# A Perceiver layer on one core: the order and the queues of the first loads

## Chip, core and metric

The kernel runs on one core of a Trainium2 chip. The metric is the device time of one execution in microseconds, as a median of several runs. A profile of one execution comes with it; its span is counted from the first to the last instruction.

## What is computed

Four batches of 256 tokens of width 256 pass through one layer with three parts, all in fp32:

```python
# x: (4, 256, 256), ctx: (4, 4096, 256)
q = layernorm(x) @ Wq1                       # 8 heads of 64
k = concat(layernorm(x) @ Wk1, ctx @ Wk2)    # 256 + 4096 keys
v = concat(layernorm(x) @ Wv1, ctx @ Wv2)
x = x + softmax(q k^T / 8) v @ Wo + bo       # cross attention
x = x + routed(layernorm(x))                 # top quarter of the tokens: attention; the others: a state space model
x = x + experts(layernorm(x))                # mixture of 8 experts, 2 per token
```

The constants spoken of below (`ln_w`, `r_w1`, `conv_w`, `A_log` and so on) belong to the routed part. The cross attention needs of the constants only its own weights and `bo`.

## The kernel before

**Cross attention in passes.** A group G is one batch and one pair of heads: 16 groups, four for each batch. For a group, the keys are made from eight chunks of ctx with 512 tokens each (`k_chunk`, L872): a load of 512 KB into one of four `ctx` buffers (L801), matmuls with `wk2` (L879) into one of three PSUM banks with tag "m", and a copy to `kt` on ScalarE (`keys_out`, L867). `k_self` (L885) adds the keys of x itself and the queries (L892, weights `wself`, held in one buffer). `v_chunk` (L902) makes the values from the same chunks of ctx, loaded a second time (L916). The norm of a batch (`norm`, L834) is done on VectorE and ScalarE, with `bo` added to `x_sb` by POOL (L842); `turn_x` (L845) transposes it on TensorE (L850) and copies it on ScalarE (L854).

**The first group.** The keys of group 0 come ahead of the loop: chunk 0, the norm of batch 0, chunks 1 to 7 with `turn_x` after chunk 4, then `k_self` (L1059 to L1066). Under `manual_schedule` each engine executes its instructions in the order in which the program writes them.

**The loop.** L1069 runs over n, 8 steps for each group: scores of step n (L932, L940), exponentials of step n - 1 on ScalarE (L980), maxima on VectorE (L952), transposes on VectorE (L989), values times weights on TensorE (L998). Between them lie pieces that make the next data: steps 2 to 4 of a group make its values (nine chunks), steps 6, 7 and 0 the keys of the next group. Loads of ctx are written at the place where the chunk is made, and SyncE's queue runs ahead of the other engines until no buffer is free. In step 0 of a group, `wk` and `wself` for the next group are loaded ahead of the first ctx chunk.

**The planner.** Work other than that is written as generators. `start(g)` puts one on a list; `slot(budget)` (L738), called three or four times in each step, lets each generator on the list go one step if the planner's clock `now[0]` has come to its due time and its cost fits in the budget. A generator yields the time to its next step and that step's cost. The clock is advanced by estimates (2.1 for the scores, 1.75 or 1.95 for a piece), not by measured times. `finish_batch` and, after it, `routed` start on this list when the fourth group of a batch has been through the loop, for batch 0 at about n = 34.

**The loads at the start.** `load_qk(0)` and `load_self(0)` go on SyncE's queue. On ScalarE's queue go x of all four batches (L809), `xbo` (L71), `xwo` (L815), and in `load_consts` (L88) 16 loads: `abo`, `r_w1`, `r_w2`, nine columns (L77), `r_b2`, `conv_w`, `xproj_w` and `A_log`. `load_consts` also computes with them (`bqs`, the exponential of `A_log`, `w2b`) and makes masks and indices on POOL. These two parts are written ahead of the `manual_schedule` block.

Of the kernel before, what the change touches and what calls it, by code (L numbers as in the profile page):

```python
# [8 lines left out]
F32 = mybir.dt.float32  # L9
# [5 lines left out]
P = 128  # L15
B, T, D = 4, 256, 256
# [27 lines left out]
def perceiver_layer(ctx: ExitStack, tc: tile.TileContext, a: dict, out: bass.AP):  # L44
# [23 lines left out]
    def row_bc(name):  # L68

        t = const.tile([P, D], F32, name=f"{name}_bc")  # L70
        nc.scalar.dma_start(out=t, in_=a[name].partition_broadcast(P))  # L71
        return t

    def col(name, n):

        t = const.tile([P, n], F32, name=f"{name}_col")
        nc.scalar.dma_start(out=t, in_=a[name].rearrange("(c p) -> p c", p=P))  # L77
        return t

    def rows(name, n, m):  # L80

        t = const.tile([P, n, m], F32, name=f"{name}_sb")
        nc.scalar.dma_start(out=t, in_=a[name].rearrange("(c p) m -> p c m", p=P))
        return t

    cs = {}

    def load_consts():  # L88

        cs["abo"] = row_bc("abo")  # L90
        cs["r_w1"] = rows("r_w1", KD, P)
        cs["r_w2"] = rows("r_w2", 1, 1)
        for name, n in (
            ("ln_w", KD), ("ln_b", KD), ("r_b1", 1), ("bq", KD), ("bk", KD), ("bv", KD),
            ("conv_b", NDT), ("dt_b", NDT), ("Dp", NDT),
        ):
            cs[name] = col(name, n)
        t = cs["r_b2"] = const.tile([P, 1], F32, name="r_b2_bc")
        nc.scalar.dma_start(out=t, in_=a["r_b2"].partition_broadcast(P))
        bqs = cs["bqs"] = const.tile([P, KD], F32, name="bqs")  # L100
        nc.vector.tensor_scalar_mul(bqs, cs["bq"], AHD ** -0.5)
        cs["conv_w"] = rows("conv_w", NDT, DC)
        cs["xproj"] = rows("xproj_w", NDT, DTR + 2 * DS)

        amat = cs["amat"] = rows("A_log", NDT, DS)
        nc.scalar.activation(amat, amat, AF.Exp)
        nc.vector.tensor_scalar_mul(amat, amat, -1.0)
        w2b = cs["w2b"] = const.tile([P, P], F32, name="w2b")
        nc.vector.tensor_copy(w2b, cs["r_w2"][:, 0, :].to_broadcast([P, P]))

        tri = cs["tri"] = const.tile([P, P], F32, name="tri")
        nc.gpsimd.affine_select(
            out=tri, in_=ones, compare_op=ALU.is_gt, fill=0.0, base=0,
            pattern=[[1, P]], channel_multiplier=-1,
        )
        tokid = cs["tokid"] = const.tile([P, 2], F32, name="tokid")
        nc.gpsimd.iota(
            tokid, pattern=[[P, 2]], base=0, channel_multiplier=1,
            allow_small_or_imprecise_dtypes=True,
        )  # L120
        posid = cs["posid"] = const.tile([P, T], F32, name="posid")
        nc.gpsimd.iota(
            posid, pattern=[[1, T]], base=0, channel_multiplier=0,
            allow_small_or_imprecise_dtypes=True,
        )

        hm1 = const.tile([P, 8], F32, name="hm1")
        hmask = cs["hmask"] = const.tile([P, 8], F32, name="hmask")
        nc.gpsimd.affine_select(
            out=hm1, in_=ones[:, :8], compare_op=ALU.is_ge, fill=0.0, base=0,  # L130
            pattern=[[-AHD, 8]], channel_multiplier=1,
        )
        nc.gpsimd.affine_select(
            out=hmask, in_=hm1, compare_op=ALU.is_gt, fill=0.0, base=AHD,
            pattern=[[AHD, 8]], channel_multiplier=-1,
        )

        vbd = cs["vbd"] = const.tile([P, AH // 2, 2, AHD], F32, name="vbd")
        nc.gpsimd.memset(vbd, 0.0)

    def moments(src):
        n = src.shape[1]
# [631 lines left out]
    with ExitStack() as s1:  # L774
# [14 lines left out]
        def load_qk(G):  # L789
            return load_weights(G, ("wk2",), "wk2", 2)  # L790

        def load_self(G):
            return load_weights(G, ("wk1", "wq1"), "wself", 1)
# [10 lines left out]
            )  # L804
            return t

        wqk, wself, wv = {0: load_qk(0)}, {0: load_self(0)}, {}
        for b in range(B):
            nc.scalar.dma_start(  # L809
                out=x_sb[:, 2 * b : 2 * b + 2, :],  # L810
                in_=a["x"][b].rearrange("(h p) d -> p h d", p=P),
            )
        bo_bc = row_bc("xbo")
        wo = fin.tile([P, NHC, D], F32, name="xwo_sb")
        nc.scalar.dma_start(out=wo, in_=a["xwo"].rearrange("(c p) m -> p c m", p=P))  # L815
        load_consts()

        same = fin.tile([P, 4, 32], F32, name="same")
        dm = same[:, 0, :]
# [52 lines left out]
        def k_chunk(G, g):  # L872
            b = G // NHP
            if G not in kts:
                kts[G] = wk.tile([P, 4, QK], F32, tag="kt", name="kt")
            ct = load_ctx(b, g)
            ps = ps_m.tile([P, 512], F32, tag="m", name="psk")
            for c in range(KD):
                nc.tensor.matmul(  # L879
                    ps, wqk[G][:, 0, c, :], ct[:, c, :],  # L880
                    start=(c == 0), stop=(c == KD - 1),
                )
            keys_out(G, g * (CK // 4), ps)
# [173 lines left out]
        with tc.manual_schedule():  # L1057
            norms = {}
            k_chunk(0, 0)  # L1059
            for _ in norm(0):  # L1060
                pass
            for g in range(1, NCH):
                k_chunk(0, g)
                if g == 4:
                    turn_x(0)
            k_self(0)  # L1066
            wv[0] = load_v(0)
            N = 8 * NG
            for n in range(N + 2):  # L1069
                G, s = divmod(n, 8)  # L1070
                new, old = n < N, 1 <= n <= N


                pieces, took = [], 1.75
                if s == 5 and G + 1 < NG:
                    wv[G + 1] = load_v(G + 1)
                if s % 4 == 1:
                    m, took = n // 4 - 1, 1.95
                    if m >= 0:
                        pieces = [  # L1080
                            lambda i=i: values(m, i, min(i + 9, NJ)) for i in range(0, NJ, 9)
                        ]
                elif 2 <= s <= 4 and G < NG:
                    pieces = [
                        lambda g=g: v_chunk(G, g) for g in range(3 * s - 6, 3 * s - 3)
                    ]
                elif G + 1 < NG:
                    if s == 0:
                        wqk[G + 1] = load_qk(G + 1)
                        wself[G + 1] = load_self(G + 1)  # L1090
                    pieces = {
                        0: [lambda g=g: k_chunk(G + 1, g) for g in range(3)],
                        6: [lambda g=g: k_chunk(G + 1, g) for g in range(3, 6)],
                        7: [lambda: k_self(G + 1)]
                        + [lambda g=g: k_chunk(G + 1, g) for g in range(6, 8)],
                    }[s]

                def piece(i):
                    if i < len(pieces):
                        pieces[i]()  # L1100
                        now[0] += took

                if new:
                    scores(n)
                    now[0] += 2.1
                if old:
                    exps(n - 1)
                if new:
                    copy_max(n)
                piece(0)  # L1110
                if s % 4 != 1:
                    slot(0.5)
                    piece(1)
                    if old:
                        turn(n - 1, 0)
                    if new:
                        stat(n)
                        now[0] += 0.3
                    if old:
                        turn(n - 1, 1)  # L1120
                    slot(0.5)
                    piece(2)
                    slot(2.9)
                else:
                    slot(1.5)
                    piece(1)
                    if new:
                        stat(n)
                        now[0] += 0.3
                    slot(2.8)  # L1130
                    piece(2)
                    slot(1.5)
                    piece(3)
                    if old:
                        turn(n - 1, 0)
                        turn(n - 1, 1)
                b = n // 32 + 1
                if b < B:
                    if n % 32 == 20:
                        norms[b] = norm(b)  # L1140
                    if n % 32 in (20, 22):
                        next(norms[b])
                    if n % 32 == 29:
                        turn_x(b)
# [443 lines left out]
```

## Time and profile before

| | us |
|---|---|
| median of 3 runs (1651.16 to 1979.53) | 1652.6 |
| profiled execution | 1654.12 |
| its span | 1652.4 |
| TensorE matmul busy | 1502.1 (91%) |
| VectorE busy | 1027.0 (62%) |
| ScalarE busy | 757.6 (46%) |
| POOL busy | 454.3 (27%) |
| mean DMA traffic | 135 GB/s |
| end of the last matmul of the first `k_self` | 42.05 |

In the profile PE is TensorE's matmul, PEld its weight load, DVE VectorE, ACT ScalarE, POOL GpSimd, SP SyncE; ACTq and SPq are the instruction queues of ScalarE and SyncE where they issue loads. L with a number is a line of the kernel. `out<-in` names the written and the read tile, `xN` counts instructions. A line of waits reads: who waited, for whom, us in total, how many times, longest. A line of the chain of waits gives start, length and what the time was spent on.

### The profile page before, as it was taken

The page shows a single profiled execution, that of the slowest core. Times are in us where ns is not written, and L with a number is a line of the kernel's source. Part 1 is how long each engine was busy: PE and PEld are TensorE (multiplying, and loading weights), DVE is VectorE, ACT ScalarE, POOL GpSimd, SP SyncE. Part 2 cuts the span into 40 slices and gives each one's busy share as a digit, 9 for nine tenths or more (in the row PEclk, how much of TensorE's full clock was granted, in tenths as well). Part 3 has the DMA queues.
Part 4 walks back from the last instruction along what each step waited for, and adds up shares of the span by engine and source line. Part 5 has one row for each costly group of instructions (what it writes and reads, how often), then busy time and mean ns, then how long its engine had stood idle before and what let it go on. Part 6 is the DMA issues. An engine that isn't in the chain of part 4 may idle for free.

```text
span 1652.4 us, 37317 instructions
## 1 busy us (share of the span) xinstructions
PE 1502.1 (91%) x15724; PEld 1079.1 (65%) x15724; DVE 1027.0 (62%) x1721; ACT 757.6 (46%) x1481; POOL 454.3 (27%) x591
## 2 busy tenths in 40 slices
PE   5899999999999999999999999999876697766799
PEld 2557667576857667686757576756654586666587
DVE  0556666567469996655899866469894313444353
ACT  2444454446566663646675445566542133222211
POOL 1000000000427871040678400427573161000110
PEclk8999999999999999999999999999987697787799
DMA  5453443443444542523454443344401364542361
GB/s 172 147 170 110 151 144 106 155 146 102 137 149 145 162 156 85 180 94 117 152 177 146 125 135 103 132 152 139 122 15 58 134 227 163 185 146 90 105 226 45
DMA packets 157687, 223.41 MB, mean 135 GB/s; under 512 B 14896, under 2 KB 76080, under 8 KB 157520
## 3 DMA queue, kind: packets, MB, share of 16 engines
q1 hardware_dynamic: 142928, 208.15, 39.0%
q10 hardware_dynamic: 13104, 8.81, 1.9%
q0 software_dynamic: 1488, 4.07, 0.8%
q8 instruction: 124, 2.03, 0.5%
q14 instruction: 43, 0.35, 0.1%
HBM read 216.56 MB, written 4.42 MB: 134 GB/s over the span
## 4 chain that ended last, share of the span: by engine, by line
PE 79%; DVE 12%; DMA 3%; issue 2%; ACT 2%; POOL 1%; SPq 1%; ACTq 0%; DVEq 0%; POOLq 0%
PE psv L916 15%; PE po L998 14%; PE su L932 13%; PE psk L879 11%; PE su L940 2%; DVE sp L952 2%; PE yps L665 2%; DMA ctx<-in_ctxT 2%; PE p1b L1403 2%; DVE db L582 2%; PE pdb L1417 2%; PE pg L1510 2%; PE pu L1510 2%; PE pde L1522 2%; DVE pt L989 2%
## 5 line engine op out<-in xcount | busy, mean ns | idle before, releaser
L952 DVE TENSOR_SCALAR_CACHE_REDUCE sp<-su 128x1088 f32<-128x1088 f32 x256 | 318.7, 1281 | 170.3 <-PE su L940 170.1
L989 DVE STREAM_TRANSPOSE pt<-sp 128x1088 f32<-128x1088 f32 x256 | 327.9, 1295 | 81.6 <-PE po L998 81.3
L980 ACT ACTIVATE sp<-sp,nb 128x1088 f32<-128x1088 f32 x256 | 305.2, 1195 | 3.8 <-DVE nb L969 3.6
L879 PE MATMUL psk<-ctx,wk 128*128 128x512 f32 x512 | 249.6, 621 | 23.2 <-ACT kt L867 9.3
L998 PE MATMUL po<-pt,v 128*64 128x128 f32 x4352 | 261.0, 278 | 3.6 <-DVE pt L989 3.5
L932 PE MATMUL su<-kt,qz 64*32 64x512 f32 x4096 | 255.1, 606 | 2.8 <-DVE nb L969 2.0
L916 PE MATMUL psv<-wv,ctx 128*128 128x128 f32 x2048 | 251.2, 279 | 0.0
L998 PEld LDWEIGHTS po<-pt,v 128*64 128x64 f32 x4352 | 242.6, 139 | 9.4 <-issue 4.7
L916 PEld LDWEIGHTS psv<-wv,ctx 128*128 128x128 f32 x2048 | 236.1, 192 | 7.8 <-issue 3.2
L879 PEld LDWEIGHTS psk<-ctx,wk 128*128 128x128 f32 x512 | 92.1, 194 | 110.8 <-issue 80.5
L920 ACT COPY v<-psv 128x512 f32<-128x512 f32 x144 | 80.3, 560 | 162.3 <-PE psv L916 161.9
L932 PEld LDWEIGHTS su<-kt,qz 64*32 64x32 f32 x4096 | 63.1, 107 | 121.5 <-issue 88.8
L589 POOL TENSOR_TENSOR db<-db,cb 128x384 f32<-128x384 f32 x96 | 106.9, 1114 | 115.5 <-DVE db L582 88.4
L582 DVE TENSOR_TENSOR_SCAN db<-da,db 128x192 f32<-128x192 f32 x192 | 136.3, 769 | 0.0
L591 POOL TENSOR_TENSOR y<-y,db 128x192 f32<-128x192 f32 x192 | 122.1, 636 | 15.1
L867 ACT COPY kt<-psk 128x512 f32<-128x512 f32 x128 | 73.8, 583 | 110.8 <-PE psk L879 110.5
L572 ACT ACTIVATE da<-delta,A_log_sb 128x192 f32<-128x192 f32 x192 | 75.9, 447 | 97.5 <-DVE db L582 95.7
L460 POOL TENSOR_SCALAR xc<-xi,conv_w_sb,conv_b_col 128x192 f32<-128x192 f32 x16 | 8.0, 497 | 390.6 <-ACT xi L492 214.1
L940 PEld LDWEIGHTS su<-kt,qz 128*32 128x32 f32 x2048 | 34.7, 110 | 109.7 <-issue 109.7
L577 POOL TENSOR_TENSOR db<-bb,xc 128x384 f32<-128x384 f32 x96 | 96.4, 1028 | 0.2
L1251 DVE SCALAR_TENSOR_TENSOR sg<-sg,p0b 128x512 f32<-128x512 f32 x19 | 13.1, 687 | 124.5 <-ACT sg L1250 124.5
L665 PE MATMUL yps<-db,ident 128*128 128x192 f32 x128 | 38.2, 466 | 49.9 <-DVE db L663 49.9
(274 smaller groups left out, 1686.3 us busy)
## 6 DMA issues: line engine op xcount, KB each, us to landing
ctx<-in_ctxT SPq DMA_DIRECT2D x256, 512.0 KB, 4.6
gateT<-in_gateT SPq DMA_DIRECT2D x27, 512.0 KB, 3.9
upT<-in_upT SPq DMA_DIRECT2D x27, 512.0 KB, 8.1
downT<-in_downT SPq DMA_DIRECT2D x27, 512.0 KB, 5.7
bb<-bcd SPq DMA_DIRECT2D x24, 192.0 KB, 4.9
cb<-bcd SPq DMA_DIRECT2D x24, 192.0 KB, 5.2
wv<-in_wv SPq DMA_DIRECT2D x32, 128.0 KB, 2.3
in_w<-in_in_w SPq DMA_DIRECT2D x24, 128.0 KB, 3.3
```

The lines of the kernel that those rows point to most:

```text
L577: nc.gpsimd.tensor_tensor(db, bbs[k], bc(xc[:, m, :], 1, SG), ALU.mult)
L582: nc.vector.tensor_tensor_scan(out=db[:, s, :], data0=da[:, s, :], data1=db[:, s, :], initial=0.0, op0=ALU.mult, op1=ALU.add,)
L589: nc.gpsimd.tensor_tensor(db, db, cbs[k], ALU.mult)
L591: nc.gpsimd.tensor_tensor(y[:, m, :], y[:, m, :], db[:, s, :], ALU.add)
L879: nc.tensor.matmul(ps, wqk[G][:, 0, c, :], ct[:, c, :], start=(c == 0), stop=(c == KD - 1),)
L916: nc.tensor.matmul(ps[:, i * P : (i + 1) * P], lhsT, wv[G][:, w, c, :], start=(c == 0), stop=(c == KD - 1),)
L920: nc.scalar.copy(v.rearrange("p k d -> p (k d)"), ps[:, : n * P])
L932: nc.tensor.matmul(su[q * 32 : (q + 1) * 32, SC[j] + lo : SC[j] + lo + 512], qT[r, j, s * 32 : (s + 1) * 32], kt[r, q, lo : lo + 512], sta ...
L952: nc.vector.tensor_scalar(out=sps[n][j], in0=su[:, SU[j] : SU[j] + QK], scalar1=1.0, scalar2=None, op0=ALU.mult, op1=ALU.max, accum_out=nm ...
L980: nc.scalar.activation(sps[n][j], sps[n][j], AF.Exp, bias=nbs[n][:, j : j + 1], accum_out=lss[b][:, hp, s, j : j + 1],)
L989: nc.vector.transpose(pts[m, j][:, i, :], sps[n][j])
L998: nc.tensor.matmul(pos[m][j * HD : (j + 1) * HD, :], vts[m // 2, k // 4][:, k % 4, j * HD : (j + 1) * HD], pts[m, j][:, :, kk * 32 : (kk + ...
```

## The change

Ahead of the first matmul only these loads are issued: `wk2` of the first pair of heads (SyncE's queue), x of batch 0 (ScalarE's queue) and ctx. `wself` follows the first ctx chunk on SyncE's queue, and `xbo` follows the first key copy on ScalarE's. x of batches 1 to 3, `xwo` and the 16 constants become a generator `load_later`, which is started on the planner's list ahead of the loop. Each of its steps issues one load on SyncE's queue, and a last step, 8 units of the planner's clock after the last load, does the arithmetic on the constants. What POOL makes is put in `make_consts`, called where `load_consts` was.

```diff
     def row_bc(name):
...
-        nc.scalar.dma_start(out=t, in_=a[name].partition_broadcast(P))
+        nc.sync.dma_start(out=t, in_=a[name].partition_broadcast(P))
...
     def col(name, n):
...
-        nc.scalar.dma_start(out=t, in_=a[name].rearrange("(c p) -> p c", p=P))
+        nc.sync.dma_start(out=t, in_=a[name].rearrange("(c p) -> p c", p=P))
...
     def rows(name, n, m):
...
-        nc.scalar.dma_start(out=t, in_=a[name].rearrange("(c p) m -> p c m", p=P))
+        nc.sync.dma_start(out=t, in_=a[name].rearrange("(c p) m -> p c m", p=P))
...
+    def make_consts():
...
     def load_consts():
 
-        cs["abo"] = row_bc("abo")
         cs["r_w1"] = rows("r_w1", KD, P)
+        yield 1.0, 0
         cs["r_w2"] = rows("r_w2", 1, 1)
+        yield 1.0, 0
         for name, n in (
             ("ln_w", KD), ("ln_b", KD), ("r_b1", 1), ("bq", KD), ("bk", KD), ("bv", KD),
             ("conv_b", NDT), ("dt_b", NDT), ("Dp", NDT),
         ):
             cs[name] = col(name, n)
+            yield 1.0, 0
         t = cs["r_b2"] = const.tile([P, 1], F32, name="r_b2_bc")
-        nc.scalar.dma_start(out=t, in_=a["r_b2"].partition_broadcast(P))
+        nc.sync.dma_start(out=t, in_=a["r_b2"].partition_broadcast(P))
+        yield 1.0, 0
+        cs["conv_w"] = rows("conv_w", NDT, DC)
+        yield 1.0, 0
+        cs["xproj"] = rows("xproj_w", NDT, DTR + 2 * DS)
+        yield 1.0, 0
+        amat = cs["amat"] = rows("A_log", NDT, DS)
+        yield 1.0, 0
+        cs["abo"] = row_bc("abo")
+        yield 8.0, 0.5
         bqs = cs["bqs"] = const.tile([P, KD], F32, name="bqs")
         nc.vector.tensor_scalar_mul(bqs, cs["bq"], AHD ** -0.5)
-        cs["conv_w"] = rows("conv_w", NDT, DC)
-        cs["xproj"] = rows("xproj_w", NDT, DTR + 2 * DS)
-
-        amat = cs["amat"] = rows("A_log", NDT, DS)
+
         nc.scalar.activation(amat, amat, AF.Exp)
         nc.vector.tensor_scalar_mul(amat, amat, -1.0)
         w2b = cs["w2b"] = const.tile([P, P], F32, name="w2b")
         nc.vector.tensor_copy(w2b, cs["r_w2"][:, 0, :].to_broadcast([P, P]))
...
-        wqk, wself, wv = {0: load_qk(0)}, {0: load_self(0)}, {}
-        for b in range(B):
-            nc.scalar.dma_start(
+        wqk, wself, wv = {0: load_qk(0)}, {}, {}
+
+        def load_x(b):
+            (nc.sync if b else nc.scalar).dma_start(
                 out=x_sb[:, 2 * b : 2 * b + 2, :],
                 in_=a["x"][b].rearrange("(h p) d -> p h d", p=P),
             )
-        bo_bc = row_bc("xbo")
+
+        load_x(0)
+        make_consts()
+        bo_bc = const.tile([P, D], F32, name="xbo_bc")
         wo = fin.tile([P, NHC, D], F32, name="xwo_sb")
-        nc.scalar.dma_start(out=wo, in_=a["xwo"].rearrange("(c p) m -> p c m", p=P))
-        load_consts()
+
+        def load_later():
+
+            for b in range(1, B):
+                load_x(b)
+                yield 2.0, 0
+            nc.sync.dma_start(out=wo, in_=a["xwo"].rearrange("(c p) m -> p c m", p=P))
+            yield 2.0, 0
+            yield from load_consts()
...
             k_chunk(0, 0)
+            wself[0] = load_self(0)
+            nc.scalar.dma_start(out=bo_bc, in_=a["xbo"].partition_broadcast(P))
             for _ in norm(0):
                 pass
...
             k_self(0)
+            start(load_later())
             wv[0] = load_v(0)
```

More of the change, by code (lines that the diff above doesn't have):

```diff
@@ L82, in rows @@
         t = const.tile([P, n, m], F32, name=f"{name}_sb")
-        nc.scalar.dma_start(out=t, in_=a[name].rearrange("(c p) m -> p c m", p=P))
+        nc.sync.dma_start(out=t, in_=a[name].rearrange("(c p) m -> p c m", p=P))
         return t
     cs = {}
-    def load_consts():
-        cs["abo"] = row_bc("abo")
[L91 to L98, printed above, removed]
-        nc.scalar.dma_start(out=t, in_=a["r_b2"].partition_broadcast(P))
-        bqs = cs["bqs"] = const.tile([P, KD], F32, name="bqs")
-        nc.vector.tensor_scalar_mul(bqs, cs["bq"], AHD ** -0.5)
-        cs["conv_w"] = rows("conv_w", NDT, DC)
-        cs["xproj"] = rows("xproj_w", NDT, DTR + 2 * DS)
-        amat = cs["amat"] = rows("A_log", NDT, DS)
[L106 to L109, printed above, removed]
+    def make_consts():
         tri = cs["tri"] = const.tile([P, P], F32, name="tri")
@@ L139, in load_consts @@
         nc.gpsimd.memset(vbd, 0.0)
+    def load_consts():
+        cs["r_w1"] = rows("r_w1", KD, P)
+        yield 1.0, 0
+        cs["r_w2"] = rows("r_w2", 1, 1)
+        yield 1.0, 0
+        for name, n in (
+            ("ln_w", KD), ("ln_b", KD), ("r_b1", 1), ("bq", KD), ("bk", KD), ("bv", KD),
+            ("conv_b", NDT), ("dt_b", NDT), ("Dp", NDT),
+        ):
+            cs[name] = col(name, n)
+            yield 1.0, 0
+        t = cs["r_b2"] = const.tile([P, 1], F32, name="r_b2_bc")
+        nc.sync.dma_start(out=t, in_=a["r_b2"].partition_broadcast(P))
[8 more added lines that the diff above has]
+        yield 8.0, 0.5
+        bqs = cs["bqs"] = const.tile([P, KD], F32, name="bqs")
+        nc.vector.tensor_scalar_mul(bqs, cs["bq"], AHD ** -0.5)
+        nc.scalar.activation(amat, amat, AF.Exp)
+        nc.vector.tensor_scalar_mul(amat, amat, -1.0)
+        w2b = cs["w2b"] = const.tile([P, P], F32, name="w2b")
+        nc.vector.tensor_copy(w2b, cs["r_w2"][:, 0, :].to_broadcast([P, P]))
     def moments(src):
```

## The prediction

> **What bounds the kernel now.** I read the page's first part, then the busy times by stretch, then the chain of waits of the first 60 us, then the timelines of the two queues that issue loads. The busy times by stretch:
>
> ```profile
> core 0: us, PE busy (x) PEld busy (x) DVE busy (x) ACT busy (x) POOL busy (x), PEclk, DMA share, GB/s
> 0.00:60.00 60.00, 36.09 (x180) 14.91 (x188) 10.24 (x29) 17.43 (x29) 4.30 (x18) 0.88 0.60 184
> 60.00:360.00 300.00, 299.20 (x3708) 204.76 (x3700) 188.38 (x297) 139.51 (x246) 2.40 (x4) 1.00 0.41 131
> ```
>
> TensorE is the bound from 60 us on (299.2 of 300 us busy). Only the first 60 us have holes, 24 us of them. The chain of waits shows what fills them:
>
> ```profile
> 4.61 8.35 DMA ctx<-in_ctxT
> ...
> 17.44 4.07 DMA ctx<-in_ctxT
> 21.51 0.02 issue
> 21.53 0.37 ACTq L83
> 21.91 0.04 issue
> 21.95 4.62 DMA A_log_sb<-in_A_log
> ...
> 40.31 1.74 PE psks L892 x8
> ```
>
> The columns are start and length in us. The first keys end at 42.05 us, and before that the chain runs over the list of constants on ScalarE's queue. That list must be issued before ScalarE can do its first copy out of PSUM, as its timeline shows:
>
> ```profile
> 8.89 1.25 ACTq L83 DMA_DIRECT2D r_w_sb<-in_r_w  x2
> ...
> 21.95 1.71 ACTq L83 DMA_DIRECT2D A_log_sb<-in_A_log  x1
> 23.68 1.28 ACT L867 ACT_TABLE_LOAD   x1 [23.68 <-DMA Dp_col<-in_Dp]
> 24.98 0.59 ACT L867 COPY kt<-psk 128x512 f32<-128x512 f32 x1
> ```
>
> The first chunk's matmuls ended at 12.76 us; their copy starts at 24.98 us. Three banks of PSUM are full by 17.44 us, and TensorE stands still from there to 25.62 us. SyncE's queue is held too; its waits up to 130 us include these:
>
> ```profile
> SPq L801 <- DMA r_w_sb<-in_r_w: 9.8, 1, 9.8
> SPq L801 <- DMA dt_b_col<-in_dt_b: 4.0, 1, 4.0
> SPq L801 <- DMA x_sb<-in_x: 3.7, 3, 1.8
> ```
>
> The issue of a ctx chunk waited for loads of the other queue to land.
>
> [...] a matmul L879 takes 0.94 us at first (4 in 3.75) and 0.44 later (12 in 5.32), the weight loads fall from 0.33 to 0.19 us after 14.02 us, and after the hole it is slow again (4 in 3.78 at 25.62 and at 30.56). [...] the trace has both queues sharing 345 to 381 GB/s between 4.5 and 8 us. [...]
>
> **The change part by part.**
>
> *Fewer bytes ahead of the first matmul.* Now it starts at 9.01 us, by when x of four batches (1024 KB), three weights (384 KB), ctx chunk 0 (512 KB) and most of a row constant (128 KB) have moved. After, it needs wk (128 KB), x of one batch (256 KB, sharing the engines) and chunk 0 (512 KB): 0.92 MB. The bandwidth in slices of 0.75 us from 1.5 us on is 28, 145, 309, 367, 360 GB/s, which sum to 0.91 MB at 5.25 us. About 0.3 us lies between the last bytes and the matmul (2.05 MB are reached near 8.7 us, the matmul starts at 9.01). Start 5.6 us: 3.4 us gained.
>
> *From the first matmul to the end of the first own keys (L892).* Now 42.05 - 9.01 = 33.0 us. After, ScalarE has one load (xbo, 0.35 us) behind the first copy. TensorE has 32 matmuls L879, four transposes and the L892 group. Of the first 12 matmuls about six were slow (3.75 + 4.43 us against 12 x 0.443 = 5.3 leaves 2.9 us excess, 0.5 each). So 6 x 0.94 + 26 x 0.443 + 0.82 + 1.74 = 19.7 us with no hole. Is it fed? ScalarE: copy 0 at 9.4 to 10.0, xbo to 10.4, square-root table 11.7, root 12.0, VectorE 0.4, two scalings 1.1 to 13.5, copy 1 to 14.1, copy 2 to 14.7. Chunk 3 needs copy 0, chunk 4 (due at 15.7) copy 1, the transposes (17.5) copy 2 and the scaled x: all in time, by 1.6 us or more. ctx: chunks 1 to 3 follow wself at about 350 GB/s, landing near 7.7, 9.6 and 11 us against 9.4, 12.1 and 13.9; chunks 4 to 7 wait for their buffer and land about 3.9 us after chunks 0 to 3 end, 13.3 at the earliest against 15.7. End: 5.6 + 19.7 = 25.3 us; 13.3 us gained here. Taken together 16.7 us.
>
> *x of batches 1 to 3 and wo on SyncE's queue.* The planner's steps put x1 and x2 between the three ctx loads of step n = 0, x3 in n = 1, wo in n = 2. Now TensorE waits at 45.1 to 46.97 us for the first of those chunks, which is late because wself, in one buffer, can only be reloaded after L892. That wait stays. Each 256 KB is 0.7 us at 370 GB/s; chunk two then lands near 48.9 us in the old time against 48.8 due, chunk three near 51.1 against 50.9: a cost of 0.3 us (0 to 1.5). x3 and wo (another 2.1 us) fall into the stretch to 62 us where SyncE has run ahead to full buffers: nothing.
>
> *Sixteen small loads, between steps n = 2 and 7.* They have 0.35 to 1.71 us of issue each or for a pair, 9.0 us in all by ScalarE's timeline, on a queue that spends 53 us of 60 to 130 us waiting:
>
> ```profile
> SPq L801 <- PE psv L916: 16.5, 3, 11.1
> SPq L801 <- PE psk L879: 13.5, 4, 8.5
> SPq L783 <- PE psv L916: 10.5, 1, 10.5
> ```
>
> These waits are for TensorE to free a buffer; they are the cover. What is behind a small load is the next ctx load: it is issued about 8.1 us ahead of its use (buffer of value chunk 0 free at 64.0, chunk 4 due at 72.1) and takes 5.6 us to land, so 2.5 us are spare. One small load's issue (0.5 us) and bytes fit. I take zero, bounds 0 and 3 us; uncovered, the 9.0 us would count in full.
>
> *The closing step* (exponential 0.26 us on ScalarE, three VectorE operations of 0.6 us together) moves to n = 8, where VectorE and ScalarE are under two thirds busy: zero, at most 0.6 us. The POOL constants move earlier on an engine that nobody waits for: zero. The planner's clock counts no time for the loads, and the list is used up before the router starts near n = 35: the later order stays.
>
> *Sum.* -3.4 - 13.3 + 0.3 = -16.4 us. The span goes from 1652.4 to 1636.0 us; the profiled run (1654.1 us) would give 1637.7. The median shown is 1652.6, 1.5 below that run, so the prediction is 1636.2 us, 1.0% faster.
>
> **The rivals.**
> 1. *A new hole in the first pass.* If the table load ahead of copy 0 only starts once chunk 0 is ready (1.3 us), the norm's ScalarE work delays copies 1 and 2 to 15.4 and 16.0 us, near their due times; a ctx chunk late by 2 us on top lets the clock fall back, and eight matmuls cost 0.5 us more each. Together 1.3 + 2 + 8 x 0.5 = 7.3 us of the gain go: 1643.5 us. For it: a short hole at 29.4 kept the clock low until 34 us. Against it: the margins above.
> 2. *SyncE's queue becomes the bound in n = 3 to 7.* If two small loads had to land (2.8 us each, as bv_col took) before the next ctx load proceeds, that load would come 5.6 + 5.6 - 8.1 = 3.1 us late; about 11 ctx loads have such neighbours, 34 us in all, and the time would be 1670 us, slower than before. It decides from a lateness of 1.5 us a chunk. For it: the 9.8 and 4.0 us waits shown. Against it: nine small loads were issued at 15.5 to 19.2 us, 0.4 to 0.5 us apart, without waiting for each other to land.
> 3. *A little more.* [...] 1 us is saved; if the hole at 54.9 to 57.7 us no longer drops it (32 matmuls L932 took 3.19 us after it, 1.88 later), another 1.3: 1634 us. Most of this is in the likeliest case's range.
>
> **How the numbers follow.** The likeliest case has 0.70 and a range of 1631 to 1641 us ([...] the x loads 1.2, spread between runs 1.5 to 3). Rival 1 has 0.15, rival 2 has 0.06, rival 3 0.06, and 0.03 is for a change in the later stages that no view shows. The range from 1628 to 1648 takes in rivals 1 and 3. Two per cent, about what a measurement can tell from no change, is 33 us. All but parts of rival 2 and of the rest lie within: faster 0.03, same 0.93, slower 0.04.
>
> **What would show it right or wrong.** Right: first matmul near 5.6 us, copy 0 near 9.4, no hole over 1 us among L879, L892 ending near 25 us, the hole before n = 1 as before, TensorE over 99% busy from 45 us on. Wrong: matmuls L879 at 0.94 us beyond the first eight; TensorE waiting for ctx with SyncE's queue held by a constant; TensorE busy below 98% between 45 and 120 us.

## The result, and the profile after

| | before | after | difference | predicted |
|---|---|---|---|---|
| median, us | 1651.2 | 1637.3 | -13.9 | -16.4 |
| ratio (95% interval) | | 0.9916 (0.9896 to 0.9936) | | 0.990 |
| first matmul of the keys, us from the start | 9.01 | 5.75 | -3.3 | -3.4 |
| end of the first own keys | 42.05 | 24.67 | -17.4 | -16.7 |
| start of the first value matmul | 62.0 | 45.8 | -16.2 | -16.4 |
| span of the profiled execution | 1652.4 | 1633.2 | -19.2 | -16.4 |

The median of before has one more run in it than the one shown with the prediction. The slow run of 1979.5 us is left out of it here, and out of the ratio. The new time lies in the predicted range (1631 to 1641 us). The change is small, 0.84%, but the interval keeps it clear of no change: it goes from 11 to 17 us.

The chain of waits of the kernel after, over the same stretch (start, length, what):

```profile
1.31 4.30 DMA ctx<-in_ctxT
5.61 0.14 issue
5.75 3.56 PE psk L902 x4
...
22.93 1.74 PE psks L915 x8
...
26.64 5.75 DMA ctx<-in_ctxT
32.39 0.14 issue
32.52 1.95 PE psk L902 x4
...
45.89 4.08 PE psv L939 x32
```

No ScalarE list stands in it any more. The one thing that is longer than before lies behind the own keys: the chain is in ctx loads until 32.39 us. The second ctx load of step n = 0 now stands behind an x load and takes 5.75 us to land, and TensorE waits for it a second time (1.1 us). ScalarE's timeline shows what the copies were freed of:

```profile
1.34 1.28 ACT L890 ACT_TABLE_LOAD   x1 [1.34 <-PEq L1602]
...
9.33 0.59 ACT L890 COPY kt<-psk 128x512 f32<-128x512 f32 x1 [6.71 <-PE psk L902]
9.34 0.39 ACTq L1084 DMA_DIRECT2D xbo_bc<-in_xbo  x1
9.94 1.28 ACT L168 ACT_TABLE_LOAD   x1
```

The first copy follows its matmuls at once (24.98 us before). The first table load runs while ScalarE has nothing else to do, so the dependence on chunk 0 that the first rival feared is not there. In the steps where the constants are issued, SyncE's queue waits for TensorE, as it did before; its longest waits up to 130 us:

```profile
SPq L812 <- PE psv L939: 34.3, 6, 14.0
SPq L812 <- PE psk L902: 19.1, 10, 4.0
```

**Why 16.2, 19.2 and 13.9 us are one gain.** At the copy of the first finished values (L1009 before, L1032 after) the gain is 16.0 us; at the tenth such copy it is 15.9 us (409.20 and 393.29). Then it grows in jumps, in steps where the two kernels have the same work, to 17.4 at the eighteenth and 18.9 at the nineteenth. Busy times in the stretch of the last of these jumps, first before, then after (the third number from the end is the granted clock of TensorE as the profile gives it, 1.00 for full speed):

```profile
717.00:766.00 49.00, 48.20 (x570) 39.18 (x576) 23.91 (x37) 27.20 (x57) 20.32 (x33) 0.97 0.34 115
```
```profile
700.00:747.00 47.00, 46.20 (x568) 37.63 (x560) 23.60 (x37) 26.86 (x57) 20.32 (x33) 1.00 0.36 120
```

TensorE idles for 0.8 us in both, and the clock was 0.97 against 1.00. By estimate, three per cent of 48 us is about 1.5 us, the whole jump. I take the jumps to belong to these two executions, though this clock is shown for the last one alone: the other executions of the changed kernel have spans of 1635.6 to 1637.0 us, two to four above the profiled one. What the traces show of the change is the 16 us of the start; the medians show 13.9, with an uncertainty of about 3.

### The profile page after: what moved, and what is told of

Its sections match the earlier page's. It is cut to its first block, busy times and chain, and to the rows that moved or that the text cites. A ratio compares the mean times of both kernels' runs of the same rounds, so it can differ in the third digit from the quotient of the medians.

```text
span 1633.2 us, 37319 instructions
## 1 busy us (share of the span) xinstructions
PE 1494.2 (91%) x15724; PEld 1075.6 (66%) x15724; DVE 1026.8 (63%) x1721; ACT 757.5 (46%) x1481; POOL 454.0 (28%) x591
## 4 chain that ended last, share of the span: by engine, by line
PE 79%; DVE 11%; DMA 4%; issue 2%; ACT 1%; POOL 1%; SPq 1%; ACTq 0%; POOLq 0%; DVEq 0%
PE psv L939 15%; PE po L1021 14%; PE su L955 13%; PE psk L902 11%; PE su L963 3%; DVE sp L975 2%; DMA ctx<-in_ctxT 2%; PE yps L676 2%; PE p1b L1429 2%; DVE db L593 2%; PE pdb L1443 2%; PE pg L1536 2%; PE pu L1536 2%; PE pde L1548 2%; DVE pt L1012 2%
## 5 line engine op out<-in xcount | busy, mean ns | idle before, releaser
L902 PE MATMUL psk<-ctx,wk 128*128 128x512 f32 x512 | 244.9, 611 | 12.5 <-DMA ctx<-in_ctxT 11.1
```

What stands on the lines that cost most here:

```text
L902: nc.tensor.matmul(ps, wqk[G][:, 0, c, :], ct[:, c, :], start=(c == 0), stop=(c == KD - 1),)
```

## The experiments

Two places are followed in each trace: the first matmul of the keys, and the start of the first value matmul, which is free of what happens in the remaining 1590 us. Each is one execution. Ratios are to runs of the kernel before that were made beside the experiment, each with its interval.

| run | first matmul | first value matmul | median, us | ratio |
|---|---|---|---|---|
| before | 9.01 | 62.0 | 1651.2 | 1 |
| after | 5.75 | 45.8 | 1637.3 | 0.9916 (0.9896 to 0.9936) |
| e1_defer_x | 6.31 | 47.5 | 1637.9 | 0.9907 (0.9891 to 0.9924) |
| e2_wself_step1 | 6.17 | 42.2 | 1629.2 | 0.9858 (0.9842 to 0.9874) |
| e3_burst | 6.43 | 54.3 | 1644.0 | 0.9945 (0.9929 to 0.9962) |
| e4_scalar_steps | 5.87 | 46.3 | 1638.5 | 0.9928 (0.9904 to 0.9952) |
| e5_x_all_first | 6.44 | 46.0 | 1638.1 | 0.9930 (0.9904 to 0.9957) |
| e6_list_after_keys | 8.86 | 63.1 | 1653.4 | 1.0006 (0.9996 to 1.0017) |
| e7_both | 5.32 | 42.3 | 1629.4 | 0.9863 (0.9846 to 0.9880) |
| e8_wself_first | 7.31 | 48.6 | 1638.9 | 0.9910 (0.9892 to 0.9927) |
| e9_wself_x_first | 9.53 | 52.2 | 1641.4 | 0.9925 (0.9909 to 0.9942) |
| e10_before_wself_step1 | 9.29 | 58.3 | 1645.1 | 0.9955 (0.9938 to 0.9972) |

### Is it enough to move the list? (e6)

```diff
-        load_consts()
...
             k_self(0)
+            load_consts()
```

> Edit of the kernel before: only the list of 16 constants (loads and arithmetic, on ScalarE's queue, in one go) is moved from the start to behind the first own keys. My theory: the list on ScalarE's queue held the first key copies, so the keys now end near 28.5 us instead of 42.1 (first matmul still near 9 us), but ScalarE then issues 9 to 17 us before it can copy the keys of the next group, so a part comes back as a hole in steps n = 0 and 1: first value matmul at 56 to 62 us, time 1646 to 1651 us. Rival, that the bytes of the start and not ScalarE's list are what counted: the keys end at 40 us or later.

The keys end at 28.0 us, so the list did hold the first copies: moving it alone takes 14 us off them. But the time is that of before. ScalarE's timeline in this run:

```profile
28.06 0.40 ACTq L71 DMA_DIRECT2D abo_bc<-in_abo  x1
...
42.25 1.28 ACT L106 ACT_TABLE_LOAD   x1 [13.15 <-DMA Dp_col<-in_Dp]
46.71 0.26 ACT L106 ACTIVATE A_log_sb<-A_log_sb 128x64 f32<-128x64 f32 x1 [3.18 <-DMA A_log_sb<-in_A_log]
46.99 1.07 ACT L865 COPY kt<-psk 128x512 f32<-128x512 f32 x2
```

Here the list with its arithmetic lasts from 28.06 to 46.97 us, 19 us, and the next copy of keys waits behind it. I had expected some of the gain to remain; all of it went. From the end of the own keys to the first value matmul it is 35.1 us against 20.0 before: 15 us are lost where 14 were gained. In one piece the list costs about as much behind the own keys as ahead of them; what makes the change pay is that it is cut up.

### One load in each step, or all at once? (e3)

```diff
-            start(load_later())
+            rest = load_later()
+            for due, cost in rest:
+                if cost:
+                    break
+            active.append([rest, 60.0, 0.5])
```

> Edit: all 20 late loads are issued in one go on SyncE's queue after the first own keys, ahead of step n = 0, instead of one in each planner step; the closing arithmetic stays near step n = 8. My theory: SyncE's queue stands idle from 16 to 24.7 us, waiting to reload wself, and the burst (about 11 us of issue) falls mostly into this gap. ctx of step 0 is then issued near 27.5 us instead of 25.6, but without x between its chunks: L939 at 46.5 us (45.8 before), the first 32 us of steps no slower, time 1638 us. Rival, that spreading the loads is what makes the change free: every load in the burst delays ctx, L939 at 54 us or later, time 1645 us or more.

I had expected 46.5 us at the value matmuls and 1638 us; it is 54.3 and 1644.0, as the rival had it. SyncE's timeline in this run:

```profile
18.30 1.80 SPq L83 DMA_DIRECT2D r_w_sb<-in_r_w  x2
...
23.68 0.37 SPq L77 DMA_DIRECT2D bk_col<-in_bk  x1
25.12 0.37 SPq L77 DMA_DIRECT2D bv_col<-in_bv  x1
...
29.27 0.50 SPq L71 DMA_DIRECT2D abo_bc<-in_abo  x1
...
32.34 11.37 SPq L812 DMA_DIRECT2D ctx<-in_ctxT  x6
```

The 20 loads last from 16.3 to 29.8 us, 13.5 us where I had counted 11, because some of them wait for earlier loads to land (from 24.05 to 25.12 us for wo). ctx of step 0 is issued at 32.34 us instead of 25.62, 6.7 us late. TensorE stands still for 9.0 us, the granted clock is 0.50 from 32 to 37.4 us and 0.62 from 37.5 to 43, and the value matmuls start 8.4 us late. So spreading matters on SyncE's queue too: these 8 us are what the planner's steps hide.

### Does it matter which queue has the constants? (e4)

```diff
-        nc.sync.dma_start(out=t, ...)      # row_bc, col, rows, r_b2
+        nc.scalar.dma_start(out=t, ...)
```

> Edit: the 16 constants are issued in the same planner steps but on ScalarE's queue instead of SyncE's (x of batches 1 to 3 and wo stay on SyncE's). My theory: their place, not their queue, gives the gain; ScalarE spends the 9 us of issue in its idle time in steps n = 2 to 7. Start of the first value matmul 45.8 us and end of the first group's values as in the changed kernel within 0.5 us, time 1637 us. Rival, that the constants on SyncE's queue cost ctx loads some time in steps n = 2 to 7: 1 to 3 us faster. Rival, that the queue is what matters: some 8 us slower.

The value matmuls start 0.5 us later, the first values are finished at 77.62 us (77.48 after), and the intervals of the two ratios overlap for the most part. Cut into steps, the constants can be on either queue. The second half of the change's description, that SyncE issues them, is not where the gain is.

### Which bytes held the first matmul? (e5, e8, e9)

e5 loads x of all batches ahead of the first matmul again, on ScalarE's queue; e8 puts wself ahead of ctx again, on SyncE's; e9 does both.

```diff
-        load_x(0)
+        for b in range(B):                 # e5, e9: on ScalarE's queue
+            load_x(b)
...
-        wqk, wself, wv = {0: load_qk(0)}, {}, {}
+        wqk, wself, wv = {0: load_qk(0)}, {0: load_self(0)}, {}    # e8, e9
```

> Edit: x of all four batches is loaded ahead of the first matmul on ScalarE's queue, as in the kernel before; everything else as changed. My theory: 768 KB more ahead of ctx chunk 0 at 350 GB/s is 2.2 us: first matmul at 8.0 us instead of 5.75, end of the first own keys at 26.9 instead of 24.7 us, and step n = 0 gets 1.1 us back since no x lies between its ctx loads: L939 at 46.9 us, time 1638 us. Rival: x on the other queue doesn't delay ctx on SyncE's, and the first matmul starts at 5.8 us.

> Edit: the changed kernel with wself of group 0 back ahead of ctx chunk 0 on SyncE's queue, as in the kernel before. Five runs with the same start as the changed kernel had their first matmul at 5.75 to 6.43 us (mean 6.1), and x of all batches on ScalarE's queue ahead of it (e5) only moved it to 6.44. My new theory: what held the first matmul before was not x on the other queue but the two weights ahead in the same queue, whose issue is 1.0 us and whose 256 KB come first: first matmul at 7.6 us, end of the first own keys about 1.5 us later than 24.7. Rival: the order on SyncE's queue doesn't count either, first matmul at 6.1 us, and what held it is xbo and wo or all of them together.

> Edit: e8 and e5 together: wself ahead of ctx chunk 0 on SyncE's queue, x of all batches on ScalarE's. Theory that wself alone counts: first matmul at 7.6 us as in e8. Rival, that the bytes of x count once the ctx load is issued late, so that both queues' bytes go ahead of it: 8.5 to 9.0 us as in the kernel before. Time in both cases 1637 to 1641 us, since ctx chunks and banks have more slack then.

Five runs with the start of the changed kernel (after, e1 to e4) begin at 5.75 to 6.43 us, mean 6.1. 768 KB of x more move this to 6.44 only, hardly outside that spread, and not to 8.0: my reason for the first term fails. wself ahead makes 7.31 us, close to the 7.6 expected. With both it is 9.53 us, 3.4 us late, more than 0.3 and 1.2 together. That is as late as with the whole start of the kernel before (8.86 to 9.29 us in before, e6 and e10), though xbo and wo come late in e9: they are not needed for it. The ctx load in e8 and e9, issued at the same moment:

```profile
2.33 4.85 DMA ctx<-in_ctxT
```
```profile
2.33 7.06 DMA ctx<-in_ctxT
```

Issued at 1.31 us, ctx lands after 5.0 us even with x of four batches on the other queue (e5). Issued at 2.33 us, when ScalarE's queue is at the last of those four x loads (they are issued from 0.81 to 2.88 us), it takes 7.1. So x of three more batches adds nothing outside the spread to a ctx load issued at 1.31 us (4.3 to 5.0 us in the five runs without them), and 2.2 us to one issued at 2.33 us (7.06 against 4.85). How the loads of the two queues came in between each other was not shown.

e5 missed at step n = 0 too. I had expected 1.1 us back, since no x stands between its ctx loads. But wo (512 KB) now stands in the place of the first x load (256 KB): the ctx load behind it takes 6.76 us instead of 5.75, and TensorE's second wait is 1.9 us instead of 1.1.

### What does step n = 0 lose, and why? (e1, e2, e7, e10)

e1 delays x of batches 1 to 3; e2 writes the reload of wself one step later; e7 is e2 with x of batch 0 behind ctx chunk 0; e10 is e2's edit in the kernel before.

```diff
+            yield 12.0, 0                              # e1, at the start of load_later
...
+                if s == 1 and G + 1 < NG:              # e2, e7, e10
+                    wself[G + 1] = load_self(G + 1)
...
                         wqk[G + 1] = load_qk(G + 1)
-                        wself[G + 1] = load_self(G + 1)
...
             k_chunk(0, 0)
+            load_x(0)                                  # e7, on SyncE's queue
```

> Edit: the generator of late loads waits 12 units of the planner's clock before its first load, so that x of batches 1 to 3 no longer lies between the ctx loads of step n = 0 but from step n = 2 on. My theory: after the change TensorE lost 1.1 us more in step n = 0 than before because each 256 KB of x stood between two ctx chunks; the second wait for ctx (1.1 us) goes, the first (1.4 us, ctx waiting behind the reload of wself) stays. First value matmul L939 at 44.7 us instead of 45.8, time about 1636 us. Rival: the 1.1 us are the clock or a bank of PSUM; then L939 starts at 45.8 us as before.

> Edit: the reload of wself for the next group is written in step 1 instead of step 0, so that the ctx loads of step 0 do not queue behind its wait for the own keys. My theory: both waits of TensorE for ctx in step n = 0 go, since SyncE's queue runs ahead while the first keys are made: L939 starts at 43.3 us instead of 45.8, time about 1634.8 us. Rival: what delays ctx is the bandwidth taken by x and wself, not the queue; then no more than 1.1 us come, L939 at 44.7 us or later.

> Edit: as e2_wself_step1, and x of batch 0 goes on SyncE's queue behind the first ctx chunk, so that only wk and ctx chunk 0 (640 KB) are ahead of the first matmul. My theory: bytes ahead of the first matmul set its start: 256 KB less is 0.7 us, first matmul at 5.1 us instead of 5.75, L939 at 42.7 us, time about 1634 us. Rival: the start is set by the latency of the ctx load, not by what shares the engines; then the first matmul starts at 5.7 us and only the 2.5 us of the other edit remain.

> Edit of the kernel before: only the reload of wself is moved from step 0 to step 1 of each group, as in e2. e2 was some 8 us faster than the changed kernel where I had expected 2.5. Theory A: the reload's wait costs in every kernel, at n = 0 (1.9 us of waiting for ctx) and where later batches begin, so the kernel before also gains, 5 to 6 us: 1646 us. Theory B: e2's gain is tied to the x loads that the change put between the ctx loads of n = 0: then here no more than 2 us come, 1650 us.

e1 missed: 47.5 us, neither the 44.7 of the theory nor the 45.8 of its rival. Its chain:

```profile
28.23 1.86 issue
30.09 5.37 PE psk L903 x8
```

The eight matmuls are now in one piece, so the second wait did go with x. But the first wait was 1.86 us long, and the granted clock after it was 0.73 (30.1 to 33 us) and 0.69 (33 to 36 us); the eight matmuls took 5.37 us where e2 needs 3.63. In e4 four matmuls took 1.97 us after a wait as long, behind the same work:

```profile
28.62 1.87 issue
30.49 1.97 PE psk L902 x4
```

For that reason e1 can't price the x loads; it shows a wait of 1.86 us with 1.7 us of slower matmuls behind it (5.37 against 3.63). No run shows what decides between the two cases.

e2 takes the cause of the first wait away. Its chain, and then SyncE's timeline:

```profile
27.54 0.36 PE su L963 x16
27.90 3.63 PE psk L902 x8
```
```profile
17.17 0.37 SPq L812 DMA_DIRECT2D ctx<-in_ctxT  x1
17.58 0.47 SPq L821 DMA_DIRECT2D x_sb<-in_x  x1
19.33 0.37 SPq L812 DMA_DIRECT2D ctx<-in_ctxT  x1
```

The first ctx load of step n = 0 is issued at 17.17 us instead of 25.62. There is no wait for ctx left at n = 0, with x still between the ctx loads, and the value matmuls start 3.6 us earlier than in the changed kernel. So what delayed ctx was its late issue, behind the wait of the reload, and not the bandwidth, as the rival had it.

The median falls by 8 us, three times what I had expected from n = 0. e10 says that this hardly depends on the change: the same edit gives the kernel before 7 us (1645.1, theory A). The reload costs at later batches as well: TensorE's waits for ctx between 64 and 1215 us come to 3.3 us in the changed kernel and 3.0 us in the kernel before, and e2 and e10 have none there. The two profiled executions of the changed kernel and of e2 are 5.7 us apart (1633.2 and 1627.5): 3.2 us at the first finished values, the rest later. The other 2.4 us of the 8 are what the profiled execution of the changed kernel lay below the median of its spans; no trace shows where they went. In e10's trace the start of the value matmuls (58.3 us against 62.0) is no measure of step n = 0: its own keys end at 39.2 us instead of 42.05 already, mainly since four of the key matmuls took 1.98 us there against 3.78.

e7 starts at 5.32 us, 0.8 us ahead of the mean of 6.1 and near the 5.1 expected. At the value matmuls it is level with e2 (42.3 and 42.2 us), as the 32 score matmuls ahead of them took 3.18 us against 2.52; at the first finished values it leads by 0.5 us (73.81 and 74.33), and the medians can't tell the two apart. e2 and e7 are the best versions: 1.4% faster than before, half a per cent faster than the change.

## Why the prediction was right, and where not

- *The bound, and what filled the first 42 us*: right. TensorE is 299.34 of 300 us busy from 43.2 us on in the kernel after; e6 shows that the list alone was 14 us of the first keys.
- *Fewer bytes ahead of the first matmul, 5.6 us*: the size was right (5.75; 6.1 on average of five runs with this start), the reason only in part, and so the size was partly luck. The step failed where it counted x of three batches as 768 KB to be taken off by the bandwidth. Neither x nor wself alone makes the difference (e5 0.3, e8 1.2 us); both together do (e9 3.4).
- *From the first matmul to the end of the own keys, 19.7 us*: measured 18.9 us (24.67 - 5.75). Four matmuls were slow (3.56 us together) instead of six, which saves 1.0 us; the four transposes took 0.44 us instead of 0.82, and the other matmuls a little less than assumed. A hole that I had excluded takes 0.95 us back: ctx chunk 4 took 5.9 us to land where 3.9 were assumed, and came at 15.26 us for a TensorE that was ready at 14.44.
- *x of batches 1 to 3 and wo, 0.3 us (0 to 1.5)*: mis-sized. From the end of the own keys to the end of the keys of step n = 0 it is 10.5 us before (52.58 - 42.05) and 11.9 us after (36.60 - 24.67): 1.4 us, at the upper bound. The chunk behind the first x load came 5.75 us after its issue, and TensorE waited 1.1 us for it. The wait before was also misread: it starts at 45.48 us, when the scores end, and not at 45.1, so it is 1.5 us long.
- *Sixteen small loads and the closing step at nothing*: right. From the start of the value matmuls to the first finished values it is 31.5 us before (93.47 - 62.0) and 31.7 after. e3 loses about 8 us when all late loads stand in one piece ahead of ctx; that is near the 9.0 that the prediction named, but for other loads at another place, partly in idle time.
- *The sum*: -16.4 us against -16.2 at the first value matmul and -13.9 between the medians. The errors of the terms, -0.8 and +1.1, cancelled, which is luck.
- *The rivals*: the first (a new hole) came as two small ones, the 0.95 us hole and the 1.4 us at n = 0, without a fall of the granted clock (1.00 from 15.26 to 25 us and from 29.5 to 40 us). The second did not happen in the change; in e3, where the loads are not spread, small loads do wait for x and wo to land (2.3 us in all) and hold ctx back. What the prediction set against it was misread a little: between 15.5 and 19.2 us eight small loads were issued, not nine, up to 0.7 us apart. Of the third, the 1 us came, as four slow matmuls instead of six; the granted clock reads 1.00 over these four and six too (9.0 to 17.5 us before, 5.7 to 14.45 after), and no run shows what makes matmuls of 0.94 us give way to those of 0.44. The slow matmuls behind the hole before n = 1 stayed (2.99 us at a clock of 0.63; 3.19 at 0.59 before).

## What to carry to other kernels

The list of 16 small loads held back ScalarE's copies that were written behind it (17 us for 0.4 MB: its loads are issued from 6.35 to 23.66 us in the kernel before), and moving the list as a whole moved the delay with it; cut into single loads between steps it cost nothing that these runs show, on either queue. Put the load that the first matmul needs at the head of its queue: with ctx issued at 1.31 us (e5) the same x loads cost 0.3 us, with ctx behind wself at 2.33 us (e9) 2.2. Then look at what a load in single buffering holds back behind it: writing one reload a step later was worth another 7 to 8 us here.

## What the runs showed that I had not expected

- Loads ahead on two queues did not add: x alone 0.3 us, wself alone 1.2 us, both 3.4 us later at the first matmul.
- A TensorE wait of 1.86 us was followed by a granted clock of 0.73 and eight key matmuls in 5.37 us in one run (e1), one of 1.87 us by four in 1.97 us in another (e4). In e1 the slower matmuls cost 1.7 us beside the wait itself.
- The same start gave first matmuls at 5.75 to 6.43 us in five runs; a ctx load of 512 KB took 4.3 to 5.0 us to land there.
